# The opening of a four-layer kernel's first layer: which transfers come first, a written order for norms and queries, and other loads moved into the attention

## The chip, the core and the metric

The kernel runs on one core of a Trainium2 chip. The metric is the device time of one execution, in microseconds, as the median of several runs. A profile is a record of one further execution, with the times of every instruction on the core's engines: PE (matmuls), PEld (the loading of a matmul's stationary operand), DVE (vector work), ACT (activations and copies), POOL (general work, and it issues transfers), SP (issues transfers only). A queue's name with a q (SPq, POOLq) stands for the part of an engine that issues. Sixteen DMA engines move the data that SP, ACT and POOL ask for.

## The reference

Four layers follow each other on x of shape 2 x 1024 x 128. Each has the form `x = x + attn(norm(x)) * silu(ffn(norm(x)))`. The change touches the start of the first layer, whose attention is a differential attention of 8 heads with depth 2 x 128:

```python
def _L0_attn_ref(X, Wq, Wk, Wv, Wo, lambda_q1, lambda_k1, lambda_q2, lambda_k2, rms_scale):
    ...
    lam1 = jnp.exp(jnp.sum(lambda_q1 * lambda_k1, axis=-1))
    lam2 = jnp.exp(jnp.sum(lambda_q2 * lambda_k2, axis=-1))
    lam = (lam1 - lam2 + LAMBDA_INIT)[None, :, None, None]
    A1 = jnp.einsum('bhqd,bhkd->bhqk', Q1, K1) * scaling
    A2 = jnp.einsum('bhqd,bhkd->bhqk', Q2, K2) * scaling
    attn = jax.nn.softmax(A1, axis=-1) - lam * jax.nn.softmax(A2, axis=-1)
    O = jnp.einsum('bhqk,bhkd->bhqd', attn, V)
    rms = jnp.sqrt(jnp.mean(O * O, axis=-1, keepdims=True) + EPS)
    O = O / rms * rms_scale
    ...
    return jnp.einsum('bne,de->bnd', O, Wo)
```

## The kernel before

**Data.** x, its norm xn (both 128 partitions x 16 tiles of rows x 128) and the transposed norm xnT (128 x 2048) stay on the core. Rows come in four groups of 512 (`NG` = 4); groups 0 and 1 are batch 0, groups 2 and 3 batch 1. `enter` handles a group: statistics and normalisation on DVE with `rsqrt` on POOL (lines 83 to 104, and 72), four PE transposes (line 139), a copy into xnT on ACT or DVE (65, 67).

**Opening.** SP issues the four groups of x, then fills two tensors in DRAM that later layers need: `blank` (three transfers, line 2039) and `slots` (23 transfers of 64 KB of zeros, line 2043). ACT issues pv and lam. POOL issues constants of later parts (bv, wm, lora), then the three weight tensors of the first layer's feed-forward (w12, hw, w3, lines 2050 to 2054), and behind them the first head's weights (line 243). Nothing pins the engines' order in the opening; a scheduler chooses it.

**A head.** `head_weights(h)` loads w (five matrices in one transfer of 640 KB; the tile has one buffer), scales Wo into `wo` on DVE, multiplies Wq by Wk into `m` and Wv by Wo into a part of `vc` (PE, lines 254 and 256, then two ACT copies), and copies the other part of `vc` on POOL. `project(h, b)` makes q from m and xnT: four matmuls of 512 columns for a batch, each into the one buffer of the PSUM pool `p_m`, each copied out by ACT.

**Attention.** The work is cut into 32 halves (8 heads x 2 batches x 2 blocks of 512 rows). In a half, `attention` makes two scores of 128 x 1024 for each of four row tiles (PE, line 292, into a pool of three buffers), takes the maximum (DVE, nm, 302), the exponential (ACT, 304), combines the two (DVE, 310 to 312) and transposes 32 x 32 blocks into tT (DVE, 316; tT has two buffers, each for two row tiles). After each second row tile, 16 transfers of 64 KB move tT to aT: ten issued by SP, six by POOL (line 323). `collect` multiplies xn by aT into pz (PE, 334) two halves later, and `outputs` finishes a half three halves later: a matmul po (352), two ACT reads, a factor f by `rsqrt` on POOL, an update of s on DVE. `beside(n)` lists what runs beside the scores of half n; `Weave.run` mixes the two lists, and PE's order is the written one (`manual_schedule`). `beside` starts `head_weights(h + 1)` at the third half of head h.

Transfers of each way of issuing share eight semaphores in turn, so a transfer waits until the one eight places earlier has landed. POOL and SP work through their instructions in order, so what stands behind a waiting transfer waits too.

Lines that the steps below touch: 83, 84, 87, 104 (norms), 139 (transposes), 225 to 236 (lambda and rms), 243 to 258 (head weights), 268 and 275 (queries), 292 to 323 (attention), 1986 to 2054 (the opening's transfers).

Of the kernel before, what the change touches and what calls it, by code (L numbers as in the profile page):

```python
# [11 lines left out]
F32 = mybir.dt.float32  # L12
BF16 = mybir.dt.bfloat16
I32 = mybir.dt.int32
AF = mybir.ActivationFunctionType
ALU = mybir.AluOpType
# [189 lines left out]
def l0_attention(k):  # L206
# [5 lines left out]
    with ExitStack() as ctx:  # L212
# [7 lines left out]
        p_z = ctx.enter_context(tc.tile_pool(name="a0pz", bufs=1, space=PSUM))  # L220
        p_m = ctx.enter_context(tc.tile_pool(name="a0pm", bufs=1, space=PSUM))


        prod = sp.tile([P, 2, H0], F32, tag="prod", name="prod", bufs=1)
        nc.vector.tensor_tensor(prod, k.lam_in[:, 0::2, :], k.lam_in[:, 1::2, :], ALU.mult)
        pl = p_m.tile([P, 512], F32, tag="mm", name="pl")
        nc.tensor.matmul(
            pl[:, : 2 * H0], lhsT=k.ones, rhs=prod.rearrange("p a h -> p (a h)"), start=True, stop=True
        )
        lam = sp.tile([P, 2, H0], F32, tag="lam", name="lam", bufs=1)  # L230
        nc.scalar.activation(lam.rearrange("p a h -> p (a h)"), pl[:, : 2 * H0], AF.Exp)
        neglam = sp.tile([P, H0], F32, tag="neglam", name="neglam", bufs=1)
        nc.vector.tensor_tensor(neglam, lam[:, 1, :], lam[:, 0, :], ALU.subtract)
        nc.vector.tensor_scalar(neglam, neglam, -LAMBDA_INIT, None, ALU.add)
        rms = sp.tile([P, 2], F32, tag="rms", name="rms", bufs=1)
        nc.vector.tensor_scalar(rms, k.pv("rms"), 1.0 - LAMBDA_INIT, None, ALU.mult)

        mats, queries = {}, {}

        def head_weights(h):  # L240

            w = wp.tile([P, 5, 2, P], F32, tag="w", name=f"w0_{h}", bufs=1)
            nc.gpsimd.dma_start(w, k.i["l0_w"][h].rearrange("p (a c d) -> p a c d", a=5, c=2))
            m = mp.tile([P, 2, P], F32, tag="m", name=f"m0_{h}")
            vc = mp.tile([P, 3, P], F32, tag="vc", name=f"vc0_{h}", bufs=3)
            mats[h] = m, vc
            nc.gpsimd.tensor_copy(vc[:, 0:2, :], w[:, 3, :, :])
            wo = mp.tile([P, 2, P], F32, tag="wo", name=f"wo0_{h}", bufs=1)
            for c in range(2):
                nc.vector.tensor_scalar(wo[:, c, :], w[:, 4, c, :], rms[:, c : c + 1], None, ALU.mult)  # L250
            yield
            pm = p_m.tile([P, 3, P], F32, tag="mm", name=f"pm0_{h}")
            for i in range(2):
                nc.tensor.matmul(pm[:, i, :], lhsT=w[:, 0, i, :], rhs=w[:, 1, i, :], start=True, stop=True)
            for c in range(2):
                nc.tensor.matmul(pm[:, 2, :], lhsT=w[:, 2, c, :], rhs=wo[:, c, :], start=(c == 0), stop=(c == 1))
            nc.scalar.activation(m, pm[:, 0:2, :], AF.Copy, scale=scaling)
            nc.scalar.copy(vc[:, 2, :], pm[:, 2, :])
            yield

        def project(h, b):

            q = qp.tile([P, 2, S], F32, tag="q", name=f"q0_{h}{b}")
            queries[h, b] = q
            for n in range(2):
                for m in range(2):
                    pq = p_m.tile([P, 512], F32, tag="mm", name=f"pq{h}{b}{m}{n}")
                    nc.tensor.matmul(  # L268
                        pq,
                        lhsT=mats[h][0][:, m, :],  # L270
                        rhs=k.xnT[:, b * S + n * 512 : b * S + (n + 1) * 512],
                        start=True,
                        stop=True,
                    )
                    nc.scalar.copy(q[:, m, n * 512 : (n + 1) * 512], pq)
                    yield

        def attention(h, b, hf, st):
# [8 lines left out]
            for t in range(4):  # L287
# [25 lines left out]

                if t % 2 == 0:
                    tT = tp.tile([P, 4, 2, 8, 32], F32, tag="tT", name=f"tT{u}{t}")
                nc.vector.transpose(  # L316
                    tT[:, :, t % 2, :, :].rearrange("p j J c -> p J j c"),
                    e[0].rearrange("p (J j a) -> p J j a", J=8, j=4),
                )
                if t % 2 == 1:  # L320
                    for i in range(4):
                        for j in range(4):
                            (nc.gpsimd if j == 3 or (i == 0 and j > 0) else nc.sync).dma_start(  # L323
                                aT[32 * j : 32 * j + 32, t - 1 : t + 1, i, :, :].rearrange("a t J c -> a t (J c)"),
                                tT[32 * i : 32 * i + 32, j, :, :, :].rearrange("a t J c -> a t (J c)"),
                            )
                yield

        def collect(b, st):
# [52 lines left out]
        def beside(n):  # L382


            out = mat = pro = z = None
            if n >= 3:
                out = outputs(*halves[n - 3], state[n - 3])
            if n < len(halves):
                h, b, hf = halves[n]
                if b == 1 and hf == 0 and h + 1 < H0:  # L390
                    mat = head_weights(h + 1)
                nh, nb = (h, 1) if b == 0 else (h + 1, 0)
                if nh < H0:
                    if hf == 0:
                        ahead[0] = project(nh, nb) if b == 0 else None
                    elif b == 1:
                        ahead[0] = project(nh, nb)
                    pro = ahead[0]
            if 2 <= n <= len(halves) + 1:
                z = collect(halves[n - 2][1], state[n - 2])  # L400
            for j in range(4):
                yield from take(out, 1)
                yield from take(z, 1)
                yield from take(pro if mat is None else mat, 1)
                yield from take(z, 1)
            yield from take(z, 1)
            yield from take(out, 1)

        ahead = [None]
        weave = Weave()  # L410
        halves = [(h, b, hf) for h in range(H0) for b in range(B) for hf in range(2)]
        state = {}
        weave.all(head_weights(0))
        weave.all(project(0, 0))
        for n in range(len(halves) + 3):
            with tc.manual_schedule(engines={mybir.EngineType.PE}):
                if n < len(halves):
                    state[n] = {"u": f"{n}"}
                    weave.run(attention(*halves[n], state[n]), beside(n), 16, 18)
# [1553 lines left out]
def recurrent_kernel(ctx: ExitStack, tc, ins, out):  # L1973
# [8 lines left out]
    k.xnT = ap.tile([P, B * S], F32, tag="xnT", name="xnT")  # L1982
    k.s = ap.tile([P, NT, D], F32, tag="s", name="s")
    xin = ins["x"].rearrange("b (t p) d -> p (b t) d", p=P)
    for g in range(NG):
        nc.sync.dma_start(k.x[:, 4 * g : 4 * g + 4, :], xin[:, 4 * g : 4 * g + 4, :])

    k.ident = cp.tile([P, P], F32, tag="ident", name="ident")
# [12 lines left out]
    )  # L2001

    pv = cp.tile([P, NPV], F32, tag="pv", name="pv")
    nc.scalar.dma_start(pv, ins["pv"])
    k.lam_in = cp.tile([P, 4, H0], F32, tag="lam_in", name="lam_in")
    nc.scalar.dma_start(k.lam_in, ins["lam"].rearrange("p (a h) -> p a h", a=4))
    bv = cp.tile([P, len(BV), D], F32, tag="bv", name="bv")
    nc.gpsimd.dma_start(bv.rearrange("p a d -> p (a d)"), ins["bv"].partition_broadcast(P))
    wm = cp.tile([P, NWM], F32, tag="wm", name="wm")
    nc.gpsimd.dma_start(wm, ins["wm"])  # L2010
    k.lora = cp.tile([RANK, P + D], F32, tag="lora", name="lora")
    nc.gpsimd.dma_start(k.lora, ins["l3_ab"])
    k.w3 = cp.tile([P, D], F32, tag="w3", name="w3_3")

    def pv_of(name, j=None):
# [18 lines left out]
    k.blank = dp.tile([P - KD, 4 * S], BF16, tag="blank", name="blank")  # L2034
    fill = cp.tile([P, D], BF16, tag="fill", name="fill")
    nc.gpsimd.memset(fill, 0.0)
    blank = k.blank.rearrange("r (a t) -> r a t", t=D)
    for r0, r1, x in ((KD, KP, fill), (KP, KM, k.ones_h), (KM, P, fill)):
        nc.sync.dma_start(blank[r0 - KD : r1 - KD], x[0 : r1 - r0, None, :].to_broadcast([r1 - r0, 4 * S // D, D]))
    k.zero = cp.tile([P, D], F32, tag="zeros", name="zeros")  # L2040
    nc.gpsimd.memset(k.zero, 0.0)
    for i in range(NS1):
        nc.sync.dma_start(k.slots[i * P : (i + 1) * P, :], k.zero)

    with tc.tile_pool(name="ln0", bufs=3) as pool, tc.tile_pool(name="lnp0", bufs=4, space=PSUM) as pp:
        for g in range(NG):
            enter(k, pool, pp, "pt", g)
    with tc.tile_pool(name="w0f", bufs=1, side="right") as wp:
        w12 = wp.tile([P, 2, FF0], F32, tag="w12", name="w12")
        nc.gpsimd.dma_start(w12, ins["l0_w12"].rearrange("p (a f) -> p a f", a=2))  # L2050
        hw = wp.tile([P, 2, 4, FF0], F32, tag="hw", name="hw")
        nc.gpsimd.dma_start(hw, ins["l0_h"].rearrange("p (l c f) -> p l c f", l=2, c=4))
        w3 = wp.tile([P, 4, D], F32, tag="w3", name="w3")
        nc.gpsimd.dma_start(w3, ins["l0_w3"].rearrange("p (c d) -> p c d", c=4))
        l0_attention(k)
        k.stacks = Stacks(k, ctx)
        l0_ffn(k, (w12, hw, w3))
# [111 lines left out]
```

## Time and profile before

| | us |
|---|---|
| median of three runs (1899.86, 1902.19, 1903.78) | 1902.19 |
| the profiled execution, its own time | 1908.33 |
| its span, first to last instruction | 1906.6 |
| first reduction of a score (DVE, line 302) | at 42.02 |
| first matmul of pz (PE, line 334) | at 79.57 |
| first head's weights: issued, first used | at 23.92, 30.32 |
| second head's weights: issued, first used | at 33.02, 37.91 |
| zero fills of slots: first and last issue | at 8.87, 43.2 |
| first transfer to aT | at 58.52 |

Times are counted from the span's start. In the timeline's lines stand start, duration, engine, line, operation, written tile, read tiles, shapes, count; brackets hold how long the engine had been idle and what ended that. In the stretches' lines stand the stretch, its length, and per engine the busy time with the number of instructions, then the granted PE clock (1.00 is full), the busy share of the DMA engines and the GB/s that they moved. A 128x512 matmul in f32 appears as two instructions. The sizes of the transfers: x 4 x 256 KB, bv 704 KB, wm 1228 KB, lora 16 KB, w12 512 KB, hw 2048 KB, w3 256 KB, a head's weights 640 KB, blank 24, 192 and 232 KB, slots 23 x 64 KB.

### The profile page before, as it was taken

How to read it: one execution, taken by the hardware profiler on the slowest of the kernel's cores; microseconds unless marked ns; L12 is line 12 of the kernel's file. 1: busy time of each engine (PE TensorE's matmuls, PEld its weight loads, DVE VectorE, ACT ScalarE, POOL GpSimd, SP SyncE). 2: the span in 40 equal slices, each digit the busy share in tenths (PEclk: the TensorE clock that was granted, in tenths of full speed). 3: DMA queues.
4: the chain of work that ended last, by engine and by line, in shares of the span. 5: the costliest groups of instructions: out<-in, count | busy, mean ns of one | idle time of the engine just before them, and what ended most of it. 6: DMA issues, size and time to landing. Idle time of an engine off the chain costs nothing.

```text
span 1906.6 us, 24480 instructions
## 1 busy us (share of the span) xinstructions
PE 1675.6 (88%) x7703; PEld 870.1 (46%) x7727; DVE 1257.5 (66%) x2597; ACT 850.9 (45%) x1849; POOL 561.7 (29%) x888
## 2 busy tenths in 40 slices
PE   4999999999999999989997598876579947999996
PEld 2344444444444444433445355544367833444442
DVE  3988888888879888873002464667763447777771
ACT  1555555555555555543213154432133333666564
POOL 2233333333333333331003442220055531112201
PEclk9999999999999999999998699986689978999998
DMA  5333333233424333332000564302044423112100
GB/s 194 97 94 76 93 89 101 72 99 86 103 68 103 84 81 79 88 89 58 0 0 1 128 179 118 76 21 64 17 104 104 100 62 78 31 50 57 38 2 12
DMA packets 114164, 142.88 MB, mean 75 GB/s; under 512 B 28324, under 2 KB 95284, under 8 KB 112292
## 3 DMA queue, kind: packets, MB, share of 16 engines
q1 hardware_dynamic: 87860, 89.13, 18.5%
q0 software_dynamic: 25840, 52.06, 11.0%
q8 instruction: 62, 1.02, 0.2%
q14 instruction: 66, 0.54, 0.1%
q10 hardware_dynamic: 336, 0.13, 0.0%
HBM read 57.53 MB, written 16.19 MB: 39 GB/s over the span
## 4 chain that ended last, share of the span: by engine, by line
PE 52%; DVE 21%; DMA 8%; ACT 6%; POOL 5%; issue 5%; SPq 2%; POOLq 0%; DVEq 0%; ACTq 0%
PE sc L292 10%; PE f0h L450 6%; PE pz L334 5%; DVE nm L302 5%; DMA aT<-tT 4%; PE o3p L699 4%; DVE tT L316 3%; DVE e L312 3%; PE st L1788 2%; PE po L352 2%; ACT e L304 2%; PE pq L268 2%; POOL aT L323 2%; SPq L323 2%; DVE nm L1758 2%
## 5 line engine op out<-in xcount | busy, mean ns | idle before, releaser
L292 PE MATMUL sc<-xnT,q 128*128 128x512 f32 x1024 | 506.3, 596 | 5.9 <-ACT e L304 5.7
L304 ACT ACTIVATE e<-sc,nm 128x1024 f32<-128x1024 f32 x256 | 285.2, 1114 | 342.3 <-DVE nm L302 264.2
L302 DVE TENSOR_REDUCE nm<-sc 128x1 f32<-128x1024 f32 x256 | 307.9, 1205 | 9.1 <-PE sc L292 9.0
L292 PEld LDWEIGHTS sc<-xnT,q 128*128 128x128 f32 x1024 | 194.3, 191 | 234.5 <-issue 189.7
L323 POOL DMA_DIRECT2D aT<-tT x384 | 205.0, 540 | 325.0 <-DVE tT L316 174.2
L334 PE MATMUL pz<-aT,xn 128*128 128x512 f32 x512 | 263.2, 599 | 3.8 <-DMA aT<-tT 3.8
L1797 ACT ACTIVATE e<-st 128x512 f32<-128x512 f32 (+3 forms) x384 | 167.6, 492 | 124.8 <-PE st L1788 99.1
L312 DVE SCALAR_TENSOR_TENSOR e<-e,c,e 128x1024 f32<-128x1024 f32 x128 | 164.1, 1282 | 3.3
L316 DVE STREAM_TRANSPOSE tT<-e 128x1024 f32<-128x1024 f32 x128 | 158.3, 1237 | 1.1 <-DMA aT<-tT 0.3
L334 PEld LDWEIGHTS pz<-aT,xn 128*128 128x128 f32 x512 | 98.2, 192 | 120.1 <-issue 111.5
L72 POOL TENSOR_TENSOR f<-fv,neg_half 128x1 f32<-128x1 f32 x128 | 82.5, 645 | 198.6 <-DVE fv L366 123.8
L1758 DVE TENSOR_REDUCE nm<-sr 128x1 f32<-128x384 f32 (+3 forms) x176 | 105.9, 636 | 36.7 <-PE sr L1750 36.3
L1788 PE MATMUL st<-qs,ks 128*128 128x512 bf16 (+3 forms) x360 | 108.2, 324 | 6.9 <-DMA qs<-nr 4.0
L352 PE MATMUL po<-vc,z 128*128 128x384 f32 x256 | 105.9, 496 | 4.9 <-ACT oc L363 2.2
L450 PE MATMUL f0h<-h,hw 128*128 128x512 f32 x256 | 110.0, 592 | 0.0
L1083 ACT ACTIVATE e<-st 128x384 f32<-128x384 f32 (+1 forms) x128 | 58.6, 477 | 111.8 <-PE st L1047 73.0
L1737 DVE TENSOR_REDUCE nf<-sf 128x1 f32<-128x512 f32 x128 | 82.6, 683 | 19.7 <-PE sf L1736 19.2
L699 PE MATMUL o3p<-e,v 128*32 128x512 f32 (+3 forms) x768 | 87.1, 499 | 0.1
L464 DVE TENSOR_TENSOR f0y<-f0o,bv 128x512 f32<-128x512 f32 x4 | 2.8, 692 | 121.3 <-PE f0o L460 121.3
L352 PEld LDWEIGHTS po<-vc,z 128*128 128x128 f32 x256 | 47.7, 191 | 70.5 <-issue 49.3
L450 PEld LDWEIGHTS f0h<-h,hw 128*128 128x128 f32 x256 | 48.6, 190 | 61.2 <-issue 61.2
L268 PE MATMUL pq<-xnT,m 128*128 128x512 f32 x128 | 69.7, 627 | 6.9 <-ACT oc L363 4.8
(396 smaller groups left out, 2557.7 us busy)
## 6 DMA issues: line engine op xcount, KB each, us to landing
aT<-tT SPq DMA_DIRECT2D x640, 64.0 KB
aT<-tT POOLq DMA_DIRECT2D x384, 64.0 KB
w<-in_l_e SPq DMA_DIRECT2D x16, 512.0 KB
qs<-parts SPq DMA_DIRECT2D x126, 64.0 KB
ks<-parts SPq DMA_DIRECT2D x42, 192.0 KB
parts<-hm SPq DMA_DIRECT2D x14, 384.0 KB
w<-in_l_w POOLq DMA_DIRECT2D x8, 640.0 KB
wd<-in_l_e SPq DMA_DIRECT2D x16, 256.0 KB
```

The costliest lines, as they stand in the source:

```text
L292: nc.tensor.matmul(ps[:, n * 512 : (n + 1) * 512], lhsT=q[:, m, hf * 512 + t * P : hf * 512 + (t + 1) * P], rhs=k.xnT[:, b * S + n * 512 : ...
L302: nc.vector.tensor_reduce(nm, ps, AX.X, ALU.max, negate=True)
L304: nc.scalar.activation(em, ps, AF.Exp, bias=nm, accum_out=(s1, s2)[m][:, t : t + 1])
L312: nc.vector.scalar_tensor_tensor(e[0], e[1], c, e[0], ALU.mult, ALU.add)
L316: nc.vector.transpose(tT[:, :, t % 2, :, :].rearrange("p j J c -> p J j c"), e[0].rearrange("p (J j a) -> p J j a", J=8, j=4),)
L323: (nc.gpsimd if j == 3 or (i == 0 and j > 0) else nc.sync).dma_start(aT[32 * j : 32 * j + 32, t - 1 : t + 1, i, :, :].rearrange("a t J c - ...
L334: nc.tensor.matmul(pz, lhsT=k.xn[:, 8 * b + J, :], rhs=st["aT"][:, :, :, J, :].rearrange("p t i c -> p (t i) c"), start=(J == 0), stop=(J ...
L352: nc.tensor.matmul(po.rearrange("p a d -> p (a d)"), lhsT=st["z"][:, t * P : (t + 1) * P], rhs=mats[h][1].rearrange("p a d -> p (a d)"), s ...
L450: nc.tensor.matmul(ph, lhsT=hw[:, l, c, j * P : (j + 1) * P], rhs=cur[:, c, cols], start=(c == 0), stop=(c == 3))
L699: nc.tensor.matmul(po[32 * i : 32 * i + 32, c0:c1], lhsT=self.v[:, kt, vc : vc + 32], rhs=es[i], start=start, stop=stop, skip_group_check= ...
L1788: nc.tensor.matmul(ps[:, n0:512], lhsT=kk[0:KR, kt // 4, i, kt % 4 * P : (kt % 4 + 1) * P], rhs=q[0:KR, c, i, n0:512], start=not diag, sto ...
L1797: nc.scalar.activation(e[:, n0:512], ps[:, n0:512], AF.Exp)
```

## The change

- SP issues groups 0 and 1 of x, pv, lam, groups 2 and 3 of x, and nothing more before the first aT. pv and lam come from SP and not from ACT.
- The first head's weights are two transfers, the first two matrices issued by ACT as its first instruction, the other three by POOL after its memsets and selects.
- The opening is written out for PE, DVE, ACT and POOL: statistics of group 0, rms and wo, the head's products, statistics of group 1, norms and transposes of groups 0 and 1, two queries, group 2, two queries, group 3, lambda. `project(0, 0)` and the transposes use the score pool's three PSUM buffers in place of `p_m` and a pool of their own.
- The second head's weights wait for half 0's last transpose (`marks[1:2]`).
- `k.head` gives loads to three halves: at n = 6 the feed-forward's weights, at 10 bv, wm and lora, at 14 the fills of blank and slots. All are issued by POOL. Each waits for a transpose (`marks[-4:-3]`), two halves earlier than n: that of the first pair of half 4, 8 or 12. On POOL they stand behind the aT transfers of that pair (the last two fills further back, at half 13).
- The slots are filled by one transfer in place of 23; the one memset of `fill` is made twice.

The calls of `after` add a wait on the instructions that are passed. Apart from these places and the names of lines, the instructions of the two kernels are the same.

```diff
+        def entering(g):
+            sl = slice(4 * g, 4 * g + 4)
+            yield from normalising(k, sp, k.x[:, sl, :], k.xn[:, sl, :])
+            pt = p_sc.tile([P, 4, P], F32, tag="sc", name=f"pt{g}")
+            for i in range(4):
+                nc.tensor.transpose(pt[:, i, :], k.xn[:, 4 * g + i, :], k.ident)
+            copy_on(nc, g % 2 == 0, k.xnT[:, g * 512 : (g + 1) * 512], pt.rearrange("p a b -> p (a b)"))
+            yield
...
         def head_weights(h):
             w = wp.tile([P, 5, 2, P], F32, tag="w", name=f"w0_{h}", bufs=1)
-            nc.gpsimd.dma_start(w, k.i["l0_w"][h].rearrange("p (a c d) -> p a c d", a=5, c=2))
+            src = k.i["l0_w"][h].rearrange("p (a c d) -> p a c d", a=5, c=2)
+            if h:
+                i = nc.gpsimd.dma_start(w, src)
+                if h == 1:
+                    after(tc, i, marks[1:2])
+            else:
+                nc.scalar.dma_start(w[:, 0:2], src[:, 0:2])
+                nc.gpsimd.dma_start(w[:, 2:5], src[:, 2:5])
+                k.small()
+                yield
+                nc.vector.tensor_scalar(rms, k.pv("rms"), 1.0 - LAMBDA_INIT, None, ALU.mult)
...
-        def project(h, b):
+        def project(h, b, pool=None):
...
-                    pq = p_m.tile([P, 512], F32, tag="mm", name=f"pq{h}{b}{m}{n}")
+                    pq = (pool or p_m).tile([P, 512], F32, tag="sc" if pool else "mm", name=f"pq{h}{b}{m}{n}")
...
-                nc.vector.transpose(
+                mark = nc.vector.transpose(
...
+                    marks.append(mark)
...
+            if n in k.head:
+                for i in k.head[n]():
+                    after(tc, i, marks[-4:-3])
...
-        weave.all(head_weights(0))
-        weave.all(project(0, 0))
+        E = mybir.EngineType
+        with tc.manual_schedule(engines={E.PE, E.DVE, E.Activation, E.Pool}):
+            weights, start, norms = head_weights(0), project(0, 0, p_sc), [entering(g) for g in range(NG)]
+            next(weights)
+            next(norms[0])
+            next(weights)
+            weave.all(weights)
+            next(norms[1])
+            next(norms[0])
+            weave.all(norms[0])
+            next(norms[1])
+            weave.all(norms[1])
+            for g in (2, 3):
+                for _ in range(2):
+                    next(start)
+                weave.all(norms[g])
+            lambdas()
...
-    for g in range(NG):
+    for g in range(2):
         nc.sync.dma_start(k.x[:, 4 * g : 4 * g + 4, :], xin[:, 4 * g : 4 * g + 4, :])
...
+    def small():
+        nc.sync.dma_start(pv, ins["pv"])
+        nc.sync.dma_start(k.lam_in, ins["lam"].rearrange("p (a h) -> p a h", a=4))
+        for g in range(2, NG):
+            nc.sync.dma_start(k.x[:, 4 * g : 4 * g + 4, :], xin[:, 4 * g : 4 * g + 4, :])
+
+    def constants():
+        yield nc.gpsimd.dma_start(bv.rearrange("p a d -> p (a d)"), ins["bv"].partition_broadcast(P))
+        yield nc.gpsimd.dma_start(wm, ins["wm"])
+        yield nc.gpsimd.dma_start(k.lora, ins["l3_ab"])
...
-    for i in range(NS1):
-        nc.sync.dma_start(k.slots[i * P : (i + 1) * P, :], k.zero)
+    def fills():
+        blank = k.blank.rearrange("r (a t) -> r a t", t=D)
+        for r0, r1, x in ((KD, KP, fill), (KP, KM, k.ones_h), (KM, P, fill)):
+            yield nc.gpsimd.dma_start(
+                blank[r0 - KD : r1 - KD], x[0 : r1 - r0, None, :].to_broadcast([r1 - r0, 4 * S // D, D])
+            )
+        yield nc.gpsimd.dma_start(
+            k.slots.rearrange("(i p) d -> p i d", p=P), k.zero[:, None, :].to_broadcast([P, NS1, D])
+        )
...
+        def feed_forward():
+            yield nc.gpsimd.dma_start(w12, ins["l0_w12"].rearrange("p (a f) -> p a f", a=2))
+            yield nc.gpsimd.dma_start(hw, ins["l0_h"].rearrange("p (l c f) -> p l c f", l=2, c=4))
+            yield nc.gpsimd.dma_start(w3, ins["l0_w3"].rearrange("p (c d) -> p c d", c=4))
+
+        k.head = {6: feed_forward, 10: constants, 14: fills}
+        k.small = small
```

More of the change, by code (lines that the diff above doesn't have):

```diff
@@ L221, in l0_attention, with lambdas @@
         p_m = ctx.enter_context(tc.tile_pool(name="a0pm", bufs=1, space=PSUM))
[L224 to L231, printed above, removed]
         neglam = sp.tile([P, H0], F32, tag="neglam", name="neglam", bufs=1)
-        nc.vector.tensor_tensor(neglam, lam[:, 1, :], lam[:, 0, :], ALU.subtract)
-        nc.vector.tensor_scalar(neglam, neglam, -LAMBDA_INIT, None, ALU.add)
         rms = sp.tile([P, 2], F32, tag="rms", name="rms", bufs=1)
-        nc.vector.tensor_scalar(rms, k.pv("rms"), 1.0 - LAMBDA_INIT, None, ALU.mult)
+        def lambdas():
+            prod = sp.tile([P, 2, H0], F32, tag="prod", name="prod", bufs=1)
+            nc.vector.tensor_tensor(prod, k.lam_in[:, 0::2, :], k.lam_in[:, 1::2, :], ALU.mult)
+            pl = p_m.tile([P, 512], F32, tag="mm", name="pl")
+            nc.tensor.matmul(
+                pl[:, : 2 * H0], lhsT=k.ones, rhs=prod.rearrange("p a h -> p (a h)"), start=True, stop=True
+            )
+            lam = sp.tile([P, 2, H0], F32, tag="lam", name="lam", bufs=1)
+            nc.scalar.activation(lam.rearrange("p a h -> p (a h)"), pl[:, : 2 * H0], AF.Exp)
+            nc.vector.tensor_tensor(neglam, lam[:, 1, :], lam[:, 0, :], ALU.subtract)
+            nc.vector.tensor_scalar(neglam, neglam, -LAMBDA_INIT, None, ALU.add)
+        def entering(g):
[6 more added lines that the diff above has]
+            yield
         mats, queries = {}, {}
@@ L246, in head_weights @@
             mats[h] = m, vc
-            nc.gpsimd.tensor_copy(vc[:, 0:2, :], w[:, 3, :, :])
             wo = mp.tile([P, 2, P], F32, tag="wo", name=f"wo0_{h}", bufs=1)
@@ L258, in head_weights @@
             nc.scalar.copy(vc[:, 2, :], pm[:, 2, :])
+            nc.gpsimd.tensor_copy(vc[:, 0:2, :], w[:, 3, :, :])
             yield
-        def project(h, b):
+        def project(h, b, pool=None):
             q = qp.tile([P, 2, S], F32, tag="q", name=f"q0_{h}{b}")
@@ L409, in l0_attention @@
         ahead = [None]
+        marks = []
         weave = Weave()
@@ L412, in l0_attention @@
         state = {}
-        weave.all(head_weights(0))
-        weave.all(project(0, 0))
+        E = mybir.EngineType
[15 more added lines that the diff above has]
+            lambdas()
         for n in range(len(halves) + 3):
-            with tc.manual_schedule(engines={mybir.EngineType.PE}):
+            with tc.manual_schedule(engines={E.PE}):
                 if n < len(halves):
@@ L2003, in recurrent_kernel @@
     pv = cp.tile([P, NPV], F32, tag="pv", name="pv")
-    nc.scalar.dma_start(pv, ins["pv"])
     k.lam_in = cp.tile([P, 4, H0], F32, tag="lam_in", name="lam_in")
-    nc.scalar.dma_start(k.lam_in, ins["lam"].rearrange("p (a h) -> p a h", a=4))
     bv = cp.tile([P, len(BV), D], F32, tag="bv", name="bv")
-    nc.gpsimd.dma_start(bv.rearrange("p a d -> p (a d)"), ins["bv"].partition_broadcast(P))
     wm = cp.tile([P, NWM], F32, tag="wm", name="wm")
-    nc.gpsimd.dma_start(wm, ins["wm"])
     k.lora = cp.tile([RANK, P + D], F32, tag="lora", name="lora")
-    nc.gpsimd.dma_start(k.lora, ins["l3_ab"])
     k.w3 = cp.tile([P, D], F32, tag="w3", name="w3_3")
@@ L2036, in recurrent_kernel @@
     nc.gpsimd.memset(fill, 0.0)
-    blank = k.blank.rearrange("r (a t) -> r a t", t=D)
-    for r0, r1, x in ((KD, KP, fill), (KP, KM, k.ones_h), (KM, P, fill)):
-        nc.sync.dma_start(blank[r0 - KD : r1 - KD], x[0 : r1 - r0, None, :].to_broadcast([r1 - r0, 4 * S // D, D]))
     k.zero = cp.tile([P, D], F32, tag="zeros", name="zeros")
-    nc.gpsimd.memset(k.zero, 0.0)
-    for i in range(NS1):
-        nc.sync.dma_start(k.slots[i * P : (i + 1) * P, :], k.zero)
-    with tc.tile_pool(name="ln0", bufs=3) as pool, tc.tile_pool(name="lnp0", bufs=4, space=PSUM) as pp:
-        for g in range(NG):
-            enter(k, pool, pp, "pt", g)
+    def small():
[3 more added lines that the diff above has]
+            nc.sync.dma_start(k.x[:, 4 * g : 4 * g + 4, :], xin[:, 4 * g : 4 * g + 4, :])
@@ new lines, in constants @@
+    def constants():
+        yield nc.gpsimd.dma_start(bv.rearrange("p a d -> p (a d)"), ins["bv"].partition_broadcast(P))
+        yield nc.gpsimd.dma_start(wm, ins["wm"])
+        yield nc.gpsimd.dma_start(k.lora, ins["l3_ab"])
+    nc.gpsimd.memset(fill, 0.0)
+    nc.gpsimd.memset(k.zero, 0.0)
+    def fills():
[6 more added lines that the diff above has]
+            k.slots.rearrange("(i p) d -> p i d", p=P), k.zero[:, None, :].to_broadcast([P, NS1, D])
+        )
@@ L2048, in recurrent_kernel @@
     with tc.tile_pool(name="w0f", bufs=1, side="right") as wp:
         w12 = wp.tile([P, 2, FF0], F32, tag="w12", name="w12")
-        nc.gpsimd.dma_start(w12, ins["l0_w12"].rearrange("p (a f) -> p a f", a=2))
         hw = wp.tile([P, 2, 4, FF0], F32, tag="hw", name="hw")
-        nc.gpsimd.dma_start(hw, ins["l0_h"].rearrange("p (l c f) -> p l c f", l=2, c=4))
         w3 = wp.tile([P, 4, D], F32, tag="w3", name="w3")
-        nc.gpsimd.dma_start(w3, ins["l0_w3"].rearrange("p (c d) -> p c d", c=4))
+        def feed_forward():
+            yield nc.gpsimd.dma_start(w12, ins["l0_w12"].rearrange("p (a f) -> p a f", a=2))
+            yield nc.gpsimd.dma_start(hw, ins["l0_h"].rearrange("p (l c f) -> p l c f", l=2, c=4))
+            yield nc.gpsimd.dma_start(w3, ins["l0_w3"].rearrange("p (c d) -> p c d", c=4))
```

## The prediction

> **What bounds the kernel now.** I read first the busy time of three stretches: up to the first scores, up to the first matmul of pz, and the rest of the attention. The columns are the stretch, its length, then busy us and count of PE, weight loads, DVE, ACT and POOL, the granted clock, the DMA share and GB/s.
>
> ```profile
> 0.00:42.00 42.00, 15.66 (x37) 8.30 (x38) 12.30 (x66) 4.93 (x9) 10.70 (x23) 1.00 0.65 212
> 42.00:79.57 37.57, 33.48 (x72) 13.58 (x72) 32.99 (x41) 20.69 (x35) 6.38 (x12) 0.95 0.25 65
> 79.57:848.00 768.43, 759.58 (x1853) 345.55 (x1852) 661.02 (x1005) 402.14 (x936) 277.79 (x495) 1.00 0.35 89
> ```
>
> From 79.57 on PE is busy for 759.58 of 768.43 us: the attention is matmuls end to end, with DVE at 86%, POOL at 36% and the DMA engines at a third. Between 42 and 79.57 DVE is nearly full too (32.99 of 37.57). Before 42 only the DMA engines work much: an opening of waits, whose end moves all that follows one for one. Its chain of waits is next (start, length, what):
>
> ```profile
> 1.86 10.64 DMA x<-in_x
> ...
> 23.92 6.35 DMA w<-in_l_w
> ...
> 33.08 2.09 PE pq L268 x2
> 35.19 0.59 ACT q L275
> 35.83 2.07 PE pq L268 x2
> 37.90 1.71 PE sc L292 x2
> 39.61 1.45 PE pq L268 x2
> 41.06 0.86 PE sc L292 x2
> ```
>
> The last x groups land at 12.5 us; head 0's weights, issued on POOL behind bv, wm, w12, hw and w3, at 30.3. Then come four queries through one PSUM buffer, each waiting for ACT. The timeline gives the landmarks:
>
> ```profile
> 42.02 1.22 DVE L302 TENSOR_REDUCE nm<-sc 128x1 f32<-128x1024 f32 x1 [3.44 <-PE sc L292]
> 46.42 1.22 DVE L302 TENSOR_REDUCE nm<-sc 128x1 f32<-128x1024 f32 x1 [3.17 <-PE sc L292]
> 48.13 1.22 DVE L302 TENSOR_REDUCE nm<-sc 128x1 f32<-128x1024 f32 x1 [0.49 <-PE sc L292]
> ```
>
> From the second reduction, 46.42, both kernels have nearly the same instruction order on PE, DVE and ACT; the exceptions are below.
>
> **The new opening, step by step.** POOL issues w[2:5] (384 KB) after its memsets (0.2 each) and two selects (0.31 each), without bv's 0.72 ahead of them: at 2.35. Landing: pv (12 KB) took 2.5 us from issue, head 1's 640 KB 4.9 (33.02 to 37.91) beside the zero fills. So 4.9 to 7.25; with x beside it I take 7.0. w[0:2], x and pv are issued between 0.8 and 3.8 and hold 1.3 MB; the opening moved 251 to 428 GB/s between 2 and 10 us, so I take each as there when asked for.
> DVE from 7.0: both wo 0.6; group 1's four bn_stats at a pitch of 0.26, aggregate and ve, 1.35, to 8.95; four xn (1.12) to 10.1, with POOL's rs (1.05) beside them; four more to 11.2. PE: the pm products (2.05) lie under this; the transposes trail xn by 0.6, so the first query starts at 11.9. Two slow queries (2.08, 2.07): 16.0. Group 2 meanwhile: copy 0.68, statistics 1.35, rs 1.15, xn 1.12, transposes, to 16.75. Two more slow queries: 20.9. Group 3's xn are ready at 19.8. Then a transpose, half a score, three transposes, the other half: 0.3 + 1.1 + 0.7 + 1.1, with PE speeding up as at 39 to 41. First reduction at 24.2; the second follows after lambda's small product, one query (0.86) and a score (1.72), some 3 later: 27.1 to 28. Against 46.42 that is 18.4 to 19.3; I take **18.7 gained**. Bounds: 12 (second rival) and 22 (w[2:5] at 4.9, and the first rival's faster queries).
>
> The speed of PE is the open row. The granted clock reads 1.00 throughout the opening, yet 128x512 matmuls between 33 and 38 us last 1.04 each and come every 0.43 from about 41: PE speeds up 10 us after it begins at 30.4, or some 4.5 after it runs unbroken from 35.83. I took the first, which leaves all four queries slow. The Trainium skill (TensorE: Matmul & The Clock Gate, Part 1) says that the array leaves half rate after about 3.4 us of sustained work. By that rule queries three and four would be fast; the trace's 4.5 agrees with it roughly, its 10 does not.
>
> **What the attention pays.**
> 1. Head 1's wo (2 x 0.3) were done in idle DVE time at 38; now they stand in the DVE-bound stretch: **0.6**. Head 1's DMA now waits for half 0's last transpose and stands behind six aT issues (3.2): it lands 5 to 6.4 after an issue 3.7 late, about 9 to 10 after the transpose, and DVE has some 11 us of work before it asks. Taken as 0; bounds 0 to 3 (wo, then pm and the scores behind it on PE).
> 2. POOL issues three loads in half 4, three in half 8 and four fills in halves 12 and 13. Behind them on POOL wait aT's transfers and f, and for f DVE's in-order update of s. The loads cost 0.52 to 0.72 each. The fills hold many runs, which these rows price (line, engine, op, count, busy us, mean ns):
>
> ```profile
> L829 POOL DMA_DIRECT2D xs<-slots_in x23 | 13.3, 578 | 10.4 <-PE f1h L839 9.0 <-DMA slots_in<-xn,posi 1.3
> L596 POOL DMA_DIRECT2D parts<-hm x2 | 1.7, 850 | 8.0 <-DVE hm L588 8.0
> ```
>
>    128 rows take 578 ns, 384 runs of 1 KB 850: 1.1 ns a run. The slot fill's 23 x 128 = 2944 runs then take 3.7 us, the blank fills' 768, 96 and 928 some 3.3 together. With the six loads, 3.6, that is 11. POOL is idle 64% of the time, which hides most; uncovered, all 11 would show. I take **1.0**, bounds 0 to 11.
> 3. Their bytes, 2.75, 1.95 and 2.0 MB, meet DMA engines that are busy for a third. At the opening's 300 GB/s each is under 10 us of a half of 25. But POOL's six of aT's 16 transfers a pair share their queue. The room: a pair transposed by 174.2 is issued on POOL by 178.0 and lands near 180.1 (2.1 in the chain), and its buffer is written again at 189.86: 10 us. I take **1.5** for the three, bounds 0 to 24 (third rival).
>
> On ACT two pairs of copies change places, and SP loses its 26 fills ahead of the first aT, which started 15 us after them: nothing, either way.
>
> Sum: 18.7 - 0.6 - 1.0 - 1.5 = **15.6**. The profiled execution took 1908.33 (the span 1906.6 and 1.7 around it) and would become 1892.7; it lies 6.1 above the median of the runs, 1902.19, from which the same gain gives **1886.6**.
>
> **Rivals.**
> *PE is fast before the third query.* Two queries at 0.86 in place of 2.08 save 2.4: 1884.2. For it: the 4.5 us above, and PE nearly unbroken from 11.9. Against: group 2's transposes wait for DVE near 16, and pairs with gaps of 0.6 stayed slow in the trace. The skill's rule above, alone, gives this case.
>
> *The first loads are late.* The last x groups took 10.64 us in the chain beside POOL's longer rows. If w[2:5] or x lands at 12.5 instead of 7.0, 5.5 of the gain go: 1892.1. Against: 2.4 MB of bv, wm and blank are out of the way.
>
> *POOL's queue stalls the attention: slower.* The third blank fill (29 rows, 928 runs, 232 KB) was issued on SP at 4.90, and SP's wait behind it ended at 32.4. At its end about one of 16 engines works:
>
> ```profile
> 28.00:29.00 1.00, 0.00 (x0) 0.00 (x0) 0.00 (x0) 0.00 (x0) 0.00 (x0) 1.00 0.07 22
> 29.00:30.00 1.00, 0.00 (x0) 0.00 (x0) 0.00 (x0) 0.00 (x0) 0.00 (x0) 1.00 0.06 23
> ```
>
> It thus runs on one engine: 27 us beside other traffic, 12 alone at 20 GB/s. Now it stands on POOL's queue ahead of aT; 27 less 10 of slack and the 4 until the next transpose is a stall of 13. The slot fills (11 us on SP, from 32.4 to 43.6) could add as much as 8 behind aT, and hw's 2 MB, if SP's packets halve its rate, 3: 24 lost, 22.5 more than I took, and 1909.1. It decides from a stall of 17 on. Against: 12 alone is inside the slack, and aT's share of that engine is small. The Trainium skill (DMA: Bandwidth & Descriptors, on why a DMA increments its semaphore by 16) has a row count of 29 on one engine when SP issues it, which the 0.07 agrees with, but says that POOL spreads some such copies over nearly all; no run here shows that yet, and by it this rival loses its largest part.
>
> *The gain is taken back.* A stretch not limited by the opening (aT's landings are in the chain several times before 130 us) swallows it: 1902. Against: nothing there waits for a fixed moment once the fills are gone.
>
> **How the numbers follow.** The forecast has 0.50, the faster PE 0.20, late loads 0.14, the swallowed gain 0.06, the stall 0.08, and 0.02 is left for a larger gain. The time is the likeliest, 1886.6, with a range of its own of 1882 to 1891. For 8 in 10 the range goes from 1879.5 (22 gained) to 1897 (late loads and 5 of stalls). A change under 0.2%, 3.8 us, about what the three runs spread over, can't be told from none: faster 0.86, same 0.06, slower 0.08.
>
> **What would show it.** Right: the first query near 12, the second reduction at 27 to 28, later landmarks of the attention shifted by 18, less 1 to 3 past halves 4, 8 and 13, and PE as full as before between them. Wrong: w[2:5] after 9 us; a second reduction after 33; DVE waiting for wo behind head 1's DMA; PE idle for more than 3 us around half 13 with DVE's transpose waiting for aT; POOL in one fill for over 5 us.

## The result and the profile after

The changed kernel took 1897.08 us (median of 18 runs, 1892.51 to 1903.48), the kernel before, run beside it, 1901.61 (18 runs, 1899.04 to 1904.87). The ratio is 0.9978, 95% interval 0.9969 to 0.9986: 4.5 us faster, where 15.6 were forecast. The profiled execution took 1896.13, its span is 1894.3.

The busy time by stretches of the kernel after, cut at the same landmarks as before (first score reduction, first matmul of pz) and then around the place where the time went. The columns are those shown of before.

```profile
0.00:22.63 22.63, 13.28 (x37) 6.62 (x37) 13.32 (x63) 5.33 (x9) 6.50 (x16) 1.00 0.27 77
22.63:60.25 37.62, 32.79 (x72) 13.82 (x73) 33.78 (x44) 20.29 (x35) 7.42 (x14) 0.95 0.28 74
60.25:360.00 299.75, 297.99 (x729) 136.26 (x730) 258.49 (x393) 158.71 (x362) 116.32 (x202) 1.00 0.41 108
360.00:400.00 40.00, 29.74 (x70) 13.31 (x69) 23.24 (x38) 12.42 (x32) 14.50 (x24) 0.87 0.58 117
400.00:840.00 440.00, 433.88 (x1054) 196.80 (x1055) 378.21 (x577) 231.55 (x544) 157.85 (x281) 1.00 0.34 87
```

The opening, 42.00 long before, is 22.63 long now, with nearly the same engine work in it (POOL's is less, 6.50 us against 10.70, since most of the transfers that it issued there have left). The second stretch keeps its length (37.62 against 37.57). From there PE is full, as before, but for one stretch of 40 us: PE is busy for 29.74 of it, at a granted clock of 0.87. The landmarks of the opening in the timeline after:

```profile
22.63 1.22 DVE L323 TENSOR_REDUCE nm<-sc 128x1 f32<-128x1024 f32 x1
26.15 1.22 DVE L323 TENSOR_REDUCE nm<-sc 128x1 f32<-128x1024 f32 x1 [2.01 <-PE sc L313]
27.86 1.22 DVE L323 TENSOR_REDUCE nm<-sc 128x1 f32<-128x1024 f32 x1 [0.49 <-PE sc L313]
```

The second reduction moved from 46.42 to 26.15: 20.3 us gained. The first reduction of each later half, before less after, shows how long that lasts: 19.8 at half 2, 19.6 at half 8, 19.2 at half 13, 18.3 at half 14, and 5.3 at half 15, from where it stays between 5.1 and 7.6 to the end of the attention, where it is 7.5. One half, from the start of half 14 to the start of half 15, takes 13.0 us away. The timeline of POOL after, in that place:

```profile
339.28 0.89 POOL L2094 DMA_DIRECT2D blank<-fill  x1
343.38 0.74 POOL L2094 DMA_DIRECT2D blank<-ones_h  x1
...
356.32 4.83 POOL L2094 DMA_DIRECT2D blank<-fill  x1 [1.12 <-issue]
360.80 3.54 POOL L344 DMA_DIRECT2D aT<-tT  x6
363.99 0.94 POOL L72 TENSOR_TENSOR f<-fv,neg_half 128x1 f32<-128x1 f32 x1
382.83 1.56 POOL L2097 DMA_DIRECT2D slots_in<-zeros  x1 [17.91 <-DMA blank<-fill]
384.38 3.24 POOL L344 DMA_DIRECT2D aT<-tT  x6
387.64 1.09 POOL L72 TENSOR_TENSOR f<-fv,neg_half 128x1 f32<-128x1 f32 x2
388.68 0.60 POOL L256 DMA_DIRECT2D w<-in_l_w  x1
```

The first fill of blank (24 rows of 32 runs) costs POOL 0.89. A run is one contiguous piece, here of 256 bytes. The third (29 rows of 32 runs, 928 runs) costs it 4.83, and POOL's next instruction that needs that transfer's semaphore starts at 382.83, 26.5 us after the issue began. The six transfers of aT at 360.80 stand behind it in POOL's queue. The pair's other ten pieces are SP's and stand in another queue. The instructions on the tile aT, and their durations in ns (least, median, most): POOL's six with their time to landing, SP's ten, and SP's ten of the pair before:

```profile
L344 POOL DMA_DIRECT2D aT<-tT x6: 885/893/900, 360.8 to 363.4; - x6
DMA to landing us min/median/max: 20.3/20.7/21.9
...
L344 SPq DMA_DIRECT2D aT<-tT x10: 585/1752/4329, 360.2 to 378.8; - x10
...
L344 SPq DMA_DIRECT2D aT<-tT x10: 586/596/622, 349.1 to 354.9; - x10
```

POOL's pieces land over 20 us after their issue, and SP's take up to 4.33 us each to issue where they took 0.6: the fill slows both queues, not only what stands behind it. DVE's waits there, from DVE's timeline:

```profile
384.51 1.25 DVE L337 STREAM_TRANSPOSE tT<-e 128x1024 f32<-128x1024 f32 x1 [9.99 <-DMA aT<-tT]
388.24 0.35 DVE L395 SCALAR_TENSOR_TENSOR s<-oc,f,s 128x128 f32<-128x128 f32 x1 [2.49 <-POOL f L72]
...
394.97 0.28 DVE L270 TENSOR_SCALAR wo<-w,rms 128x128 f32<-128x128 f32 x1 [2.35 <-DMA w<-in_l_w]
```

and PE's, from its timeline, with a stretch of five us after its wait (the granted clock is the third number from the end):

```profile
380.45 1.02 PE L313 MATMUL sc<-xnT,q 128*128 128x512 f32 x2
381.31 1.02 PE L356 MATMUL pz<-aT,xn 128*128 128x512 f32 x2
391.54 3.78 PE L313 MATMUL sc<-xnT,q 128*128 128x512 f32 x4 [9.21 <-ACT e L325]
395.11 1.92 PE L356 MATMUL pz<-aT,xn 128*128 128x512 f32 x2
...
390.00:395.00 5.00, 3.46 (x4) 1.51 (x5) 1.90 (x6) 2.93 (x7) 0.56 (x1) 0.50 0.68 221
```

The transpose can't overwrite tT before the sixteen pieces of the pair that it holds have left it: 9.99 us. POOL's factor f, which also had to wait for POOL, keeps DVE for another 2.49. Behind DVE, ACT's exponentials and PE's score buffers run dry: PE stands still for 9.21 us, and its next matmuls run at half pace (four in 3.78; two took 1.02 before the gap), with a granted clock of 0.50. Head 5's weights, issued behind all this at 388.68, then hold DVE for 2.35.

### The profile page after: what moved, and what is told of

It is laid out like the page before. It is cut to its first block, busy times and chain, and to the rows that moved or that the text cites. A ratio compares the mean times of both kernels' runs of the same rounds, so it can differ in the third digit from the quotient of the medians.

```text
span 1894.3 us, 24447 instructions
## 1 busy us (share of the span) xinstructions
PE 1671.0 (88%) x7703; PEld 867.8 (46%) x7727; DVE 1258.0 (66%) x2597; ACT 851.8 (45%) x1849; POOL 569.1 (30%) x893
## 3 DMA queue, kind: packets, MB, share of 16 engines
q0 software_dynamic: 27232, 53.82, 11.9%
q8 instruction: 62, 1.02, 0.2%
## 4 chain that ended last, share of the span: by engine, by line
PE 46%; DVE 24%; DMA 9%; issue 6%; ACT 6%; POOL 5%; SPq 3%; POOLq 0%; DVEq 0%; ACTq 0%
PE sc L313 7%; DVE nm L323 6%; PE f0h L491 6%; DMA aT<-tT 5%; DVE tT L337 4%; PE pz L356 4%; PE o3p L740 4%; DVE e L333 3%; SPq L344 3%; PE st L1829 2%; ACT e L325 2%; DVE nm L1799 2%; PE po L374 2%; POOL aT L344 1%; PE sr L1791 1%
## 5 line engine op out<-in xcount | busy, mean ns | idle before, releaser
L1778 DVE TENSOR_REDUCE nf<-sf 128x1 f32<-128x512 f32 x128 | 82.5, 683 | 19.1 <-PE sf L1777 18.6
```

## The experiments

Theory "shape": the third fill's 29 rows make it slow on POOL's queue, whatever is beside it, and all 13 us hang on that. Rivals: its 928 runs cost that in any arrangement; the bytes of halves 12 to 14 crowd the DMA engines; only what is queued behind it matters. Ratios below are against the kernel before, run in the same series.

### The third fill as 24 and 5 rows

```diff
-        for r0, r1, x in ((KD, KP, fill), (KP, KM, k.ones_h), (KM, P, fill)):
+        for r0, r1, x in ((KD, KP, fill), (KP, KM, k.ones_h), (KM, KM + 24, fill), (KM + 24, P, fill)):
```

> The third fill of blank goes out as 24 rows and then 5 rows, the same 928 runs on the same queue at the same place. Theory 'shape' (the one transfer of 29 rows holds POOL's queue until it lands, 26 us after its issue, and aT and the slots' semaphore are late behind it): the 24 rows behave as the first fill did (0.89 us on POOL), half 15 starts with the 18 us of gain that half 14 had, and the time falls by about 13 us, to 1884 (0.991 of the kernel before). Rival 'runs' (928 runs of 256 bytes cost POOL's queue what they cost, in one piece or two): the two still take 4 to 5 us on POOL and land 20 us or more after the issue, 1894 to 1897. Rival 'traffic' (all the fills and the slots together fill the DMA engines in halves 13 and 14): no change, 1897, and aT late by the same 10 us.

Measured: 1880.44 us, ratio 0.9888 (0.9869 to 0.9907), 3.6 under the time forecast. The group of fills, by line and tile (range of the durations in ns, first and last start in us):

```profile
L2094 POOL DMA_DIRECT2D blank<-fill x3: 734/884/887, 339.9 to 365.0; - x3
```

In the kernel after, the same line has two fills of 887 and 4833. Half 15 starts 18.4 us ahead of before, half 14 starts 17.7 ahead. Nothing of the 13 is left, so neither the runs nor the bytes made it.

### The third fill as 116 rows of 8 runs

```diff
-        for r0, r1, x in ((KD, KP, fill), (KP, KM, k.ones_h), (KM, P, fill)):
+        for r0, r1, x in ((KD, KP, fill), (KP, KM, k.ones_h)):
...
+        yield nc.gpsimd.dma_start(
+            blank[KM - KD : P - KD].rearrange("r (b a) t -> (r b) a t", a=8), fill[0:116, None, :].to_broadcast([116, 8, D])
+        )
```

> The third fill as one transfer of 116 source rows with 8 runs each: the same bytes and the same 928 runs, on the same queue at the same place. Theory 'shape': 116 rows of 8 runs are dealt out in large pieces, the transfer lands within 8 us, the time falls to about 1884. Rival 'runs': one transfer of 928 runs takes POOL 4.8 us again and lands after 20 us or more, 1895 to 1897. Rival 'traffic': 1897.

Measured: 1882.81 us, ratio 0.9910 (0.9891 to 0.9929). POOL's timeline has the same 928 runs in one transfer at 1.95 us:

```profile
355.41 1.95 POOL L2097 DMA_DIRECT2D blank<-fill  x1
```

Half 15 starts 20.5 us ahead. One transfer of 928 runs is harmless when they are cut into other rows.

### The third fill on SP

```diff
-            yield nc.gpsimd.dma_start(
+            yield (nc.sync if r0 == KM else nc.gpsimd).dma_start(
```

> The third fill is issued by SP instead of POOL, at the same place. Theory 'shape': on SP the 29 rows go to one DMA engine (before, one engine ended 27 us and more after the others), so POOL's aT and slots are free, but SP's own aT pieces on that engine wait behind the fill: half 15 still loses 8 to 13 us, 1892 to 1897. Rival 'queue' (only what stands behind the fill in POOL's queue is late): the loss goes to the 4.9 us of SP's issue or less, 1885 to 1888.

Measured: 1876.99 us, ratio 0.9877 (0.9860 to 0.9893); run again in a later series, 1879.39, ratio 0.9865 (0.9843 to 0.9887). Both forecasts were too slow: the loss of 8 to 13 that theory 'shape' foresaw on SP did not come, nor the rival's of up to 4.9. SP issued the fill at 340.9 in 0.75 us, earlier than POOL's turn came. The gain is 18.8 at half 13, 16.5 at half 14 and 18.8 again at half 15; such a dip of 2 also stands at halves 20 and 30, where there is no fill. On SP nothing urgent stood behind the fill: the next aT piece was due 8.6 us later, and took 4.72 us to issue. That only what is queued behind the fill decides is not shown by this, since the same transfer is also a shorter one on SP (the fills by themselves, below).

### All fills back in the opening, on SP

```diff
-            yield nc.gpsimd.dma_start(
+            yield nc.sync.dma_start(
...
-        yield nc.gpsimd.dma_start(
+        yield nc.sync.dma_start(
...
-        k.head = {6: feed_forward, 10: constants, 14: fills}
-        k.small = small
+        k.head = {6: feed_forward, 10: constants}
+        k.small = lambda: (small(), list(fills()))
```

> All four fills go back to SP in the opening, behind the loads of x; the rest of the change stays. Theory 'shape': the loss of 13 at half 15 goes away, and the opening, whose transfers all stand ahead of the fills, keeps its 20 us; at most 2 to 4 us are lost where head 1's w or the first aT meet the fill's one engine: 1882 to 1888. Rival 'the opening gains because the fills left it': the second score reduction moves from 26 to 32 us or later and the time is 1890 or more.

Measured: 1881.54 us, ratio 0.9899 (0.9882 to 0.9915), half a microsecond under the range expected. The second reduction stays at 26.11, the gain is 18.1 at half 15 and 18.6 at the end of the attention. The opening's gain never needed the fills to leave it: behind the loads of x, where they also stood before the change, they cost it nothing. The end of the attention lies as early as with the third fill alone on SP (18.5 there), so the 4.5 us by which this kernel is slower than that one arise later; no run tells where.

### The fills by themselves

The kernel writes the constant rows to one scratch array, each transfer after the landing of the one before:

```diff
+    by32(nc.gpsimd, 24)
+    by32(nc.gpsimd, 29)
+    by32(nc.gpsimd, 28)
+    by32(nc.gpsimd, 30)
+    by32(nc.gpsimd, 5)
+    by32(nc.gpsimd, 32)
+    by8(nc.gpsimd, 116)
+    by32(nc.gpsimd, 29)
...
+    by32(nc.gpsimd, 29)
+    for i in range(60):
+        nc.sync.dma_start(a[:, 4 * (i % 4) : 4 * (i % 4) + 4, :], xin[:, 4 * (i % 4) : 4 * (i % 4) + 4, :])
+    by32(nc.gpsimd, 24)
```

> This kernel computes nothing of the reference: it writes the fill's constant rows to a scratch array, one transfer after the other, each waiting for the landing of the one before, on a chip that does nothing else, and zeros as its output. On POOL: rows 24, 29, 28, 30, 5, 32 (of 32 runs each), 116 rows of 8 runs, 29; on SP: 24, 29, 28, 116 of 8, 29; then POOL's 29 and 24 beside a stream of 256 KB loads on SP. Theory 'shape': POOL's 29 rows keep POOL over 4 us and land 15 us or more after their issue with nothing beside them, 24, 28 and 32 rows and 116 rows of 8 runs land within 6 us; SP's 29 rows run on one DMA engine for 13 to 17 us, SP's others do not. Rival 'traffic': alone, POOL's 29 rows land within 6 us like the 24, and are slow beside the loads only.

The list of DMA issues of that kernel (count, size, median us from issue to landing). 232 KB are 29 rows, and the median of four holds the 116 short rows too; 192 KB are 24 rows, 256 are 32, 240 are 30, 224 are 28, 40 are 5:

```profile
blank<-fill POOLq DMA_DIRECT2D x4, 232.0 KB, 26.9
...
blank<-fill POOLq DMA_DIRECT2D x2, 192.0 KB, 4.2
blank<-fill POOLq DMA_DIRECT2D x1, 256.0 KB, 3.3
blank<-fill POOLq DMA_DIRECT2D x1, 240.0 KB, 3.5
blank<-fill POOLq DMA_DIRECT2D x1, 224.0 KB, 3.4
...
blank<-fill POOLq DMA_DIRECT2D x1, 40.0 KB, 3.8
```

29 rows land after 26.9 us with nothing beside them; 28 and 30 rows, a little less and a little more of the same, after 3.4 and 3.5. What POOL's queue (q0, software_dynamic) moved for one transfer, in packets, MB and share of 16 engines, for 29 rows, 28 rows and 116 short rows:

```profile
q0 software_dynamic: 944, 0.29, 27.2%
...
q0 software_dynamic: 80, 0.23, 31.0%
...
q0 software_dynamic: 256, 0.25, 27.8%
```

For nearly the same bytes 29 rows take 944 packets and 28 rows 80, and the 116 short rows, whose time lies between, 256: the slow transfer is one that was cut small. POOL's timeline has their issue times, 28 rows, then later 116 short rows, then 29 rows:

```profile
33.07 0.80 POOL L27 DMA_DIRECT2D blank<-fill  x1 [22.34 <-DMA blank<-fill]
...
48.36 1.91 POOL L30 DMA_DIRECT2D blank<-fill  x1 [2.85 <-DMA blank<-fill]
57.12 4.80 POOL L27 DMA_DIRECT2D blank<-fill  x1 [6.85 <-DMA blank<-fill]
```

The 116 rows land after 8.2 (48.36 to 56.56), not within the 6 expected. Stretches of the same kernel (POOL is the second busy column; the last two are DMA share and GB/s): 29 rows on POOL, 29 rows on SP, 28 rows on SP, then 29 rows on POOL beside a stream of loads on SP, and that stream alone.

```profile
57.10:84.10 27.00, 0.00 (x0) 4.80 (x1) 1.00 0.27 11
87.50:102.00 14.50, 0.00 (x0) 0.00 (x0) 1.00 0.07 16
102.30:105.50 3.20, 0.00 (x0) 0.00 (x0) 1.00 0.33 72
134.00:154.00 20.00, 0.00 (x0) 0.00 (x0) 1.00 0.70 90
159.00:179.00 20.00, 0.00 (x0) 0.00 (x0) 1.00 0.95 277
```

On SP the 29 rows take 14.5 us at a DMA share of 0.07, one engine of 16. On POOL they keep more than four engines' worth of time busy (0.27 of 16) and still move less, 11 GB/s. Beside them all that moves, SP's stream included, is 90 GB/s, where the stream alone moves 277. The fill is slow by itself, and it slows the other queue; "traffic" is out.

### The other loads back in the opening, behind w[2:5]

This and the next three stand on the third fill on SP, so that they are compared with its 1877.0 and 1879.4.

```diff
-        k.head = {6: feed_forward, 10: constants, 14: fills}
-        k.small = small
+        k.head = {14: fills}
+        k.small = lambda: (small(), list(constants()), list(feed_forward()))
```

> With the third fill on SP as in c_sp, the six loads of constants and of the feed-forward's weights (over 4 MB) go back to POOL's queue in the opening, behind w[2:5]. Theory 'weights first': what stands ahead of them keeps its times (wo at 7, first query at 12), x of groups 2 and 3 comes some us later and takes 1 to 5 us, since PE transposes group 2 between the queries: 1877 to 1883. Rival 'the loads had to leave': the second score reduction moves from 26 to 35 or later, 1887 or more.

Measured: 1889.10 us, ratio 0.9936 (0.9914 to 0.9957): 10 to 12 us lost (11 to 13 by the ratios, as the series ran on different chips), nearer to the rival, though the second reduction, at 33.86, is not as late as it had it. The stretches of this kernel and the place where PE stops, from its timeline:

```profile
10.00:15.00 5.00, 5.00 (x12) 2.54 (x12) 2.51 (x8) 1.17 (x2) 0.80 (x1) 1.00 1.06 434
15.00:20.00 5.00, 0.59 (x2) 0.00 (x0) 0.65 (x3) 0.59 (x1) 0.00 (x0) 0.86 0.92 365
```

```profile
12.27 3.31 PE L289 MATMUL pq<-xnT,m 128*128 128x512 f32 x4
22.82 1.15 PE L245 MATMUL pt<-ident,xn 128*128 128x128 f32 x4 [7.23 <-DVE xn L104]
23.77 3.62 PE L289 MATMUL pq<-xnT,m 128*128 128x512 f32 x4
```

The first query keeps its time. Then the six loads fill the DMA engines (share 1.06 and 0.92 against 0.00 and 0.01 in the kernel after), x of group 2 is late, and PE waits 7.23 us for its norm and comes back at half pace: the third and fourth query take 3.62 together.

### The six loads ahead of w[2:5], as before

```diff
-        k.head = {6: feed_forward, 10: constants, 14: fills}
+        k.head = {14: fills}
         k.small = small
+        list(chain(constants(), feed_forward()))
```

> With the third fill on SP as in c_sp, the six loads go back into the opening ahead of w[2:5] on POOL's queue, as before; the set order stays. Theory 'transfers': w[2:5] lands at 25 to 32 instead of 7, the first query at 30 to 37, the second reduction at 43 to 50, and 17 to 23 us of the gain go: 1894 to 1900, no better than the kernel before by 0.4%. Rival 'order': the set order alone keeps half of the gain, 1888 or less.

Measured: 1893.72 us, ratio 0.9962 (0.9950 to 0.9975). DVE's wait for the weights:

```profile
20.43 0.63 DVE L270 TENSOR_SCALAR wo<-w,rms 128x128 f32<-128x128 f32 x2 [12.37 <-DMA w<-in_l_w]
```

wo starts at 20.43 instead of 6.98, the first query at 25.46 instead of 11.86, the second reduction comes at 39.76. That is 3 earlier than the theory had it, and the time is just under its range. The edit does not bring back the opening of before: POOL issues all six loads and then w[2:5] in one row, w[2:5] at 5.36, where the kernel before issued the first head's weights at 23.92. With the rest of the change kept, 7 us of gain are left; putting w[2:5] ahead of the six loads gives some 5 more, taking these out of the opening 10 to 12 more.

### The opening's set order dropped

```diff
-        with tc.manual_schedule(engines={E.PE, E.DVE, E.Activation, E.Pool}):
+        with ExitStack():
```

> With the third fill on SP as in c_sp, the opening's set order is dropped: the scheduler orders PE, DVE, ACT and POOL there, the transfers stay in their order. It puts the first groups' transposes and their copy ahead of the weights' product and m. Theory 'transfers': the order of the loads makes the gain, the set order is worth 1 to 4 us: second reduction at 27 to 30, 1878 to 1882. Rival 'order': without it the second reduction comes at 35 or later, 1886 or more.

Measured: 1878.95 us, ratio 0.9872 (0.9847 to 0.9897); the second reduction comes at 25.45, before the 26.12 of the kernel with the set order. The written order is worth nothing that can be measured here; the order of the transfers makes the gain.

### All four queries first, the second batch's norms inside the attention

```diff
-            for g in (2, 3):
-                for _ in range(2):
-                    next(start)
-                weave.all(norms[g])
+            for _ in range(4):
+                next(start)
...
+            if n == 0:
+                pro = rest()
...
+        def rest():
+
+            for g in (2, 3):
+                next(norms[g])
+                next(norms[g])
+                yield
+                for _ in norms[g]:
+                    pass
+                yield
```

> On top of c_sp: all four first queries stand ahead of the norms of groups 2 and 3, whose transposes go into the first half's attention, and batch 1's queries into the second half. Theory 'clock': PE idles less between 15 and 20 us, but the scheduler still puts the norms' DVE work ahead of the first reduction, so that it comes at 20 to 22 instead of 22.6 and the second at 23 to 25 instead of 26: 1 to 2 us less than c_sp run beside it. Rival 'nothing': DVE decides and the second half pays for batch 1's queries: as c_sp or up to 3 us slower.

> c_sp again, to be compared with k_order on the same chip: 1875 to 1880.

Measured: 1878.97 us, ratio 0.9860 (0.9832 to 0.9888), beside 1879.39 for the kernel without it: the rival 'nothing' holds. The first reduction comes at 18.91, 3.7 earlier, but by the first reduction of half 3 no more than 18.4 of gain over the kernel before is there, 1 to 2 less than in the two runs without the edit. The second half now holds batch 1's queries, and in the half after it DVE waits 2.0 us for head 1's weights; where the rest goes was not traced. Gain in the opening can be given back two halves later.

## Why the prediction was wrong

**The opening: right, a little too low.** w[2:5] was to be there at 7.0, and DVE used it at 6.98. The first query was forecast for 11.9 and began at 11.86. Group 2's transposes ended at 17.2 (16.75 reckoned). The second reduction came at 26.15 instead of 27.1 to 28, because queries three and four took 1.88 together (17.05 to 18.93) instead of 2 x 2.08. So the rival "PE is fast before the third query" was right in its mechanism: 20.3 gained, not 18.7. Not all of the 2.3 saved there arrives, since PE then waits 1.31 for group 3's norm. By the rule of the Trainium skill (TensorE: Matmul & The Clock Gate, Part 1), half rate ends after some 3.4 us of sustained work. The first two queries ran slow from 11.86 to 15.32, 3.5 us, and the next two ran fast, which agrees in kind but does not show the figure: PE had been at its transposes without a gap from 9.57, and the first two queries took 2.43 with the six loads ahead of w[2:5] and 3.78 without the set order. In the kernel with the six loads behind w[2:5], where PE waited 7.23 us in between, queries three and four ran slow, as after the wait of 9.21 us in the attention.

**Head 1's wo, 0.6: right.** From the second reduction to half 4 the gain falls from 20.3 to 19.5, 0.8.

**Two bounds do not follow from their terms.** 18.7 less 5.5 is 13.2, not 12, and with 2.1 and 2.4 on top it is 23.2, not 22; 22 gained would give 1883.3 after the three costs, not 1879.5. Nothing measured hangs on them.

**The six loads in the attention: right, cheap.** With hw's 2 MB, issued in half 4, the gain does not fall; behind the constants, issued at the end of half 8, it falls by 0.5. What the forecast did not price is what they cost in the opening: out of it they are worth 10 to 12 us of the change's gain.

**The failed step: "I take 1.5 for the three", the bytes and aT's queue.** The room of 10 us that aT had was near: here it is some 8, from POOL's last issue at 364.34 with 2.1 to land, to 374.52, when DVE was free for the transpose. But the third fill held POOL's queue for 26 us and slowed SP's pieces beside it, and the half that met it lost 13.0 instead of a part of 1.5. The sign written down for this came: PE idle for 9.21 us, with DVE's transpose waiting for aT. The term before it, POOL's issues, rested on a price of 1.1 ns a run: right for the first fill (0.89 for 768 runs), high for the slots (1.56 for 2944, where 3.7 was reckoned), and far too low for the third (4.83 for 928). With the 0.9 that half 13 lost, the two terms cost 14.4 with the constants instead of 2.5; 20.3 - 0.8 - 14.4 leaves 5.1, which is what the landmarks show from half 16 on and near the 4.5 of the medians. That last nearness proves little: at the end of the attention the landmarks show 7.5, and the two profiled executions differ by 12.2, so some us arise behind the attention that no step here prices.

**The rival "POOL's queue stalls the attention" had the path of its main part, and its size partly by luck:** 27 us on the queue and a stall of 13, where 26 and 13.0 were measured. But the 27 was SP's time on one engine beside other traffic, while POOL's 26 came from a transfer cut into many packets on more than one engine; and DVE's wait for aT was 9.99 of the 13.0, with f (2.49) and head 5's weights (2.35) late behind it. The rival was given 0.08 for two reasons. Its time also held 8 for the slots and 3 for hw, neither of which came, so that it was written as slower than before; alone, its main part in place of the 1.5 gives 15.6 - 11.5 = 4.1, about what was measured. And what was said against it was wrong: "12 alone" is SP's time for this transfer (14.5 with its issue and landing in the kernel of fills only), not POOL's 26.9. The Trainium skill (DMA: Bandwidth & Descriptors, on why a DMA increments its semaphore by 16) says that the number of engines follows the divisors of the outer sizes, with POOL spreading some copies over nearly all. The SP rows agree (0.07 for 29 rows, 0.33 for 28), and POOL's 29 rows did use more than one engine; but the inference drawn from it, that the rival then loses its largest part, failed: spread out, the transfer took nearly twice as long as on one engine.

**Shown and not shown.** That the shape of this one transfer costs the 13 us is shown by the two kernels that cut it otherwise on the same queue, and by the fills alone. The packets go with it (944 against 80); why POOL cuts 29 rows so small and 28 and 30 not is open. How the 13 us divide between POOL's queue and the slowed queue of SP is open too, since no run has one without the other. In the opening the order of the transfers is shown to matter; the three PSUM buffers of the first queries and the split of the first head's weights were in every one of these kernels and have no price.

## What to carry to other kernels

Before a transfer moves to another queue, price it on that queue, alone, in its own shape: here a price from its bytes, or from its run count by other rows, was far too low. Ask what stands behind it in that queue and how long that can wait; the same fill on SP, where nothing was due for 8.6 us, was free. The remedy costs a line: 24 and 5 rows, 116 short rows, or the other queue give 1877 to 1883 us, 18 to 25 us of gain where the change as it stands gave 4.5.

## What the runs showed of the hardware

- POOL's transfer of 29 rows of 32 runs of 256 bytes: 4.8 us of POOL, 944 packets and 26.9 to landing, alone; 28 rows 0.80, 80 packets and 3.4, 30 rows 0.79 and 3.5.
- Such a transfer slows what another queue moves: beside it all traffic was 90 GB/s, where SP's stream alone moved 277, and in the attention SP's issues of aT took up to 4.33 us instead of 0.6.
- On SP the same 29 rows use about one engine (DMA share 0.07 over 14.5 us), and SP's next issue waits for it: the first aT piece behind it took 4.72 us to issue instead of 0.6.
- A gap of 7.23 or 9.21 us on PE was paid twice: the matmuls after it ran at half pace (after 9.21, four halves of a score in 3.78 us where two take 1.02, at a granted clock of 0.50).
